# Attention and two quantized convolutions on one core: emitted instruction order, shared single PSUM banks, earlier residual loads

## The chip, the cores and the metric

The kernel runs on one core of a Trainium2 chip. The metric is the device time of one execution in microseconds (us), the median of several runs. A profile is one execution recorded by the hardware profiler; its span runs from the first instruction to the last. The engines are TensorE (PE: matmuls; PEld: its weight loads), VectorE (DVE), ScalarE (ACT), GpSimd (POOL) and SyncE (SP), which issues most transfers. Each takes its own queue of instructions, in the order in which they stand there.

## The reference, cut to what matters

Input `x` is 4 images of 128 channels of 64x64 float32. The first layer is self-attention with four heads of 32 over the 4096 pixels of each image, the second a residual block of two quantized 3x3 convolutions with batch norm.

```python
# layer 0, per image b
x_norm = group_norm(x)                       # 8 groups of 16 channels
q, k, v = split(qkv_w @ x_norm + qkv_b)      # 4 heads, d = 32, 4096 tokens
attn = softmax(q @ k.T * 32 ** -0.5)         # 4096 x 4096 per head
y0 = x + proj_w @ (attn @ v) + proj_b

# layer 1
out = conv3x3(y0, lsq_quantize(w1))          # 128 -> 128 channels, pad 1
out = relu(batchnorm(out))                   # statistics over batch and pixels
out = conv3x3(out, lsq_quantize(w2))
out = relu(batchnorm(out) + y0)              # y0 is the residual
```

## The kernel before: the parts that matter

Attention is cut into 32 blocks of 512 queries (8 for each image, or batch), and a block into 32 steps of 128 keys. One step needs four score matmuls (one for each head, two in a "pair"), two exponentials on ScalarE (128x1024 each), and four weighting matmuls that add the four heads into one PSUM bank, `acc`, each head in 32 of its partitions. The row sums of the exponentials are kept as running sums: 24 steps of a block are added by VectorE into `rsum`, 7 by accumulating transfers into `msum`, whose tiles have one buffer each.

```python
pss = tile_pool(name="pss", bufs=3, space=PSUM)      # score tiles of two banks; later convolution tiles
psa = tile_pool(name="psa", bufs=1, space=PSUM)      # single banks: tag "acc", tag "m"
ppool = tile_pool(name="ppool", bufs=6)              # p, the exponentials of one step
rpool = tile_pool(name="rpool", bufs=1)              # running sums, av, rc
MOVED = range(0, NK - 4, 4)                          # NK = 32
...
def scores(pair):
    ...
    s = pss.tile([P, 2, FB], F32, tag="s")
    for i in range(2):
        h = 2 * half + i
        nc.tensor.matmul(s[:, i, :], k[:, h, c0 : c0 + P], q[:, h, :], start=True, stop=True)
    nc.scalar.activation(pts[step][:, 2 * half : 2 * half + 2, :], s, AF.Exp, scale=SCALE)

def weights(step):
    ...
    if kt == 0:
        acc[n] = psa.tile([P, FB], F32, name=f"acc{n}", tag="acc")
    for h in range(HEADS):
        nc.tensor.matmul(acc[n][h * D : (h + 1) * D, :], v[:, kt % KB, h * D : (h + 1) * D],
                         pt[:, h, :], start=(kt == 0), stop=(kt == NK - 1))
    if kt in MOVED:
        if kt == 0:
            msum[n] = rpool.tile([P, HEADS, FB], F32, tag="rm")
            nc.sync.dma_start(out=msum[n], in_=pt)
        else:
            nc.gpsimd.dma_start(out=msum[n], in_=pt, accum_op=ALU.add)
    elif kt == 2:
        rsum[n] = rpool.tile([P, HEADS, FB], F32, tag="r")
        nc.vector.tensor_tensor(rsum[n], pts[step - 1], pt, ALU.add)
    elif kt > 2:
        nc.vector.tensor_tensor(rsum[n], rsum[n], pt, ALU.add)
```

The program emits three score pairs and one step of weights, then three pairs and two steps, over and over (`for s, w in ((3, 1), (3, 2))`). Side work is hung on the steps of a block: the row sum and output projection of the block before, and, in chunks of 512 pixels, the q, k, v projections that a later block needs.

```python
if before:                                   # the block before
    add(2, "a", before["total"])             # row sum: 8 matmuls into a bank, copied by ScalarE
    for j in range(4):
        add(4 + j, "", lambda j=j: before["invert"](j))
    add(8, "", before["weigh"])
    add(10, "q", before["project"])
    add(11, "", before["store"])
...
def chunk(b, j, kt, fs, loads):              # "q": right after a group of score pairs
    add(kt, "", fs[0])                       # normalize: xn, ScalarE
    add(kt, "q", fs[1])                      # pk matmul
    add(kt + 1, "", fs[2])                   # kh (ScalarE), kl (VectorE), two stores
    add(kt + 1, "q", fs[3])                  # pq matmul
    add(kt + 2, "", fs[4])                   # qh, ql, two stores
    add(kt + 2, "q", fs[5])                  # pv matmuls
    add(kt + 3, "", fs[6])                   # v evacuated and stored
```

Block 0 has 5 such chunks, the other blocks of images 0 to 2 have 24; three more come ahead of block 0. This text is what the program emits. In the kernel before, a scheduler then chooses the order in which instructions stand in each engine's queue.

The convolutions split each input into a high and a low part and add nine shifted matmuls for each. They work on bands of 16 rows with a row at either side; two halves of 8 rows make a band.

```python
def conv(parts, ps, j, w):
    hi, lo = parts
    for part in (lo, hi):
        for tap in range(TAPS):
            nc.tensor.matmul(ps[:, j, :]..., w[:, tap, :], part[:, ...], ...)
...
        prepare(m)
        nc.scalar.copy(dst, ps[:, j, :])
        nc.vector.bn_stats(st[:, b * NB + c, :], dst)
...
a2, c2 = layer(1, second, [])
for b in range(B):
    for j in range(4):
        r = outs.tile([P, Q], F32, tag="r")
        nc.sync.dma_start(out=r, in_=y0[b][:, cs])
        y = outs.tile([P, Q], F32, tag="y")
        nc.vector.scalar_tensor_tensor(y, cv[b][:, cs], a2, r, ALU.mult, ALU.add)
        nc.scalar.activation(y, y, AF.Relu, bias=c2)
        nc.sync.dma_start(out=out[b]...[:, cs], in_=y)
```

Of the kernel before, what the change touches and what calls it, by code (L numbers as in the profile page):

```python
# [22 lines left out]
P = 128  # L23
# [44 lines left out]
def _fast(tc, x, norm_w, norm_b, qkv_wt, qkv_b, proj_wt, proj_b,  # L68
          w1, alpha1, gamma1, beta1, w2, alpha2, gamma2, beta2, out, outer):
    flag = outer.enter_context(tc.tile_pool(name="flag", bufs=1))  # L70
    cnt = flag.tile([1, 1], I32, name="cnt")
    with ExitStack() as ctx:
        _fast_body(ctx, tc, x, norm_w, norm_b, qkv_wt, qkv_b, proj_wt, proj_b,
                   w1, alpha1, gamma1, beta1, w2, alpha2, gamma2, beta2, out, cnt)
    return tc.nc.values_load(cnt[0:1, 0:1], min_val=0, max_val=P)


def _fast_body(ctx, tc, x, norm_w, norm_b, qkv_wt, qkv_b, proj_wt, proj_b,
# [116 lines left out]
    dram = ctx.enter_context(tc.tile_pool(name="dram", bufs=1, space=bass.MemoryType.DRAM))  # L195
    kpool = ctx.enter_context(tc.tile_pool(name="kpool", bufs=NB + 1))
    pss = ctx.enter_context(tc.tile_pool(name="pss", bufs=3, space=PSUM))
    psa = ctx.enter_context(tc.tile_pool(name="psa", bufs=1, space=PSUM))
    y0 = [dram.tile([P, N], F32, name=f"y0_{b}") for b in range(B)]
    att = ExitStack()  # L200
    vpool = att.enter_context(tc.tile_pool(name="vpool", bufs=NB + 1))
# [9 lines left out]
    def f32(t):  # L211
        return t.bitcast(F32)
# [12 lines left out]
    def norm_parts(b, st):  # L225
        mv = small.tile([P, 2], F32, name=f"mv{b}", tag="mv")
        mean = small.tile([P, 1], F32, name=f"mean{b}", tag="mean")
        dv = small.tile([P, 1], F32, name=f"dv{b}", tag="dv")
        gm = {}


        def one():
            nc.vector.bn_aggr(mv, st.rearrange("p j s -> p (j s)"))
            gm[0] = psa.tile([P, FB], F32, name=f"gm{b}", tag="m")
            nc.tensor.matmul(gm[0][:, 0:1], gavg, mv[:, 0:1], start=True, stop=True)

        def two():
            nc.vector.tensor_copy(mean, gm[0][:, 0:1])
            nc.vector.tensor_tensor(dv, mv[:, 0:1], mean, ALU.subtract)
            nc.vector.tensor_tensor(dv, dv, dv, ALU.mult)  # L240
            nc.vector.tensor_tensor(dv, dv, mv[:, 1:2], ALU.add)

        def three():
            gm[1] = psa.tile([P, FB], F32, name=f"gv{b}", tag="m")
            nc.tensor.matmul(gm[1][:, 0:1], gavg, dv, start=True, stop=True)

        def four():
            r = rsqrt_eps(gm[1][:, 0:1], f"gr{b}")
            a = small.tile([P, 1], F32, name=f"ga{b}", tag="ga")
            nc.vector.tensor_tensor(a, r, nw, ALU.mult)  # L250
            c = small.tile([P, 1], F32, name=f"gc{b}", tag="gc")
            nc.vector.tensor_tensor(c, mean, a, ALU.mult)
            nc.vector.tensor_tensor(c, nb, c, ALU.subtract)
            norm[b] = a, c

        return one, two, three, four


# [4 lines left out]
    def project_parts(b, j, xin, wide=False):  # L263
        xn = xpool.tile([P, FB], F32, name=f"xn{b}_{j}", tag="x")
        kq[b, j] = dram.tile([5, P, FB], F32, name=f"kq{b}_{j}")
        ps = {}

        def bank(what):
            if wide:
                t = pss.tile([P, 2, FB], F32, name=f"p{what}{b}_{j}", tag="s")  # L270
                return t[:, 0, :]
            return psa.tile([P, FB], F32, name=f"p{what}{b}_{j}", tag="m")

        def normalize():
            a, c = norm[b]
            nc.scalar.activation(xn, xin(), AF.Identity, bias=c, scale=a)

        def mm(what, o):
            ps[what] = bank(what)
            nc.tensor.matmul(ps[what], wqkv[:, o : o + P], xn, start=True, stop=True)  # L280

        def parts(what, bias, slot):
            hi = stage.tile([P, FB], F32R, name=f"{what}h{b}_{j}", tag=f"{what}h")
            lo = stage.tile([P, FB], F32R, name=f"{what}l{b}_{j}", tag=f"{what}l")
            nc.scalar.activation(hi, ps[what], AF.Identity, bias=bias)  # L285
            nc.vector.scalar_tensor_tensor(lo, ps[what], bias, f32(hi), ALU.add, ALU.subtract)  # L286
            nc.sync.dma_start(out=kq[b, j][slot], in_=f32(hi))
            nc.sync.dma_start(out=kq[b, j][slot + 1], in_=f32(lo))

        def mmv():  # L290
            ps["v"] = bank("v")
            for i in range(KB):
                nc.tensor.matmul(ps["v"][:, i * P : (i + 1) * P], xn[:, i * P : (i + 1) * P],  # L293
                                 wqkv[:, 2 * P : 3 * P], start=True, stop=True)

        def evac_v():
            v = stage.tile([P, FB], F32, name=f"vst{b}_{j}", tag="v")
            nc.vector.tensor_tensor(v.rearrange("p (i f) -> p i f", f=P),
                                    ps["v"].rearrange("p (i f) -> p i f", f=P),
                                    bv.unsqueeze(1).to_broadcast([P, KB, P]), ALU.add)  # L300
            nc.sync.dma_start(out=kq[b, j][4], in_=v)

        return [normalize, lambda: mm("k", P), lambda: parts("k", bk, 0),
                lambda: mm("q", 0), lambda: parts("q", bq, 2), mmv, evac_v]
# [39 lines left out]
    def weights(step):  # L344
        n, kt = divmod(step, NK)
        v = vs[blocks[n][0], kt // KB]
        pt = pts[step]
        if kt == 0:
            acc[n] = psa.tile([P, FB], F32, name=f"acc{n}", tag="acc")
        for h in range(HEADS):  # L350
            nc.tensor.matmul(acc[n][h * D : (h + 1) * D, :], v[:, kt % KB, h * D : (h + 1) * D],  # L351
                             pt[:, h, :], start=(kt == 0), stop=(kt == NK - 1))
        if kt in MOVED:
            if kt == 0:
                msum[n] = rpool.tile([P, HEADS, FB], F32, name=f"rm{n}", tag="rm")
# [4 lines that stand above are left out]
            rsum[n] = rpool.tile([P, HEADS, FB], F32, name=f"r{n}", tag="r")  # L360
# [4 lines that stand above are left out]
    def finish_parts(n):  # L365
# [8 lines left out]


        def total():
            t["l"] = psa.tile([P, FB], F32, name=f"l{n}", tag="m")
            for r in (msum[n], rsum[n]):
                for h in range(HEADS):
                    nc.tensor.matmul(t["l"][h * D : (h + 1) * D, :], ones, r[:, h, :],  # L380
# [14 lines left out]
            t["x"] = load_x(b, qb)  # L395

        def project():
            t["o"] = psa.tile([P, FB], F32, name=f"po{n}", tag="m")
            nc.tensor.matmul(t["o"], wp, av, start=True, stop=True)  # L399

        def store():
# [174 lines left out]
    def conv(parts, ps, j, w):  # L576
        hi, lo = parts
        n = 0
        for part in (lo, hi):
            for tap in range(TAPS):  # L580
                kh, kw = divmod(tap, 3)
                nc.tensor.matmul(ps[:, j, :].rearrange("p (r w) -> p r w", w=W), w[:, tap, :],  # L582
# [24 lines left out]
    nc.vector.tensor_reduce(big, worst, AX.X, ALU.max)  # L607
    bad = small.tile([P, 1], F32, name="bad")
    nc.vector.tensor_scalar(bad, big, LIMIT, None, ALU.is_gt)
    nbad = psa.tile([P, FB], F32, name="nbad", tag="m")  # L610
    nc.tensor.matmul(nbad[0:1, 0:1], bad, ones[:, 0:1], start=True, stop=True)
    nc.vector.tensor_copy(cnt, nbad[0:1, 0:1])
    att.close()

    mid = ctx.enter_context(tc.tile_pool(name="mid", bufs=1))
    outs = ctx.enter_context(tc.tile_pool(name="outs", bufs=4))
    cv = [mid.tile([P, N], F32, name=f"cv{b}") for b in range(B)]

    def batch_norm(i, st):
# [13 lines left out]
    def layer(i, prepare, done):  # L633

        st = mid.tile([P, B * NB, 6], F32, name=f"st{i}")
        for m, (b, g) in enumerate(bandlist):
            ps = done[m] if m < len(done) else conv_tile(i, b, g)
            for j in range(2):
# [4 lines left out]
                c = 2 * g + j  # L643
                dst = cv[b][:, c * FB : (c + 1) * FB]
                nc.scalar.copy(dst, ps[:, j, :])  # L645
                nc.vector.bn_stats(st[:, b * NB + c, :], dst)  # L646
        return batch_norm(i, st)

    def first(m):
# [4 lines left out]

    a1, c1 = layer(0, first, early)

    def relu_band(b, g):
        t = band_tile(f"t1_{b}_{g}")
        inner, lo, hi = border(t, g)
        nc.scalar.activation(inner, cv[b].rearrange("p (h w) -> p h w", w=W)[:, lo:hi, :], AF.Relu,  # L660
                             bias=c1, scale=a1)
        ready[1, b, g] = split(t, f"1_{b}_{g}")

    relu_band(*bandlist[0])
    relu_band(*bandlist[1])

    def second(m):
        if m + 2 < len(bandlist):
            relu_band(*bandlist[m + 2])

    a2, c2 = layer(1, second, [])
    Q = N // 4
    for b in range(B):
        for j in range(4):
            cs = slice(j * Q, (j + 1) * Q)
            r = outs.tile([P, Q], F32, name=f"r{b}_{j}", tag="r")
            nc.sync.dma_start(out=r, in_=y0[b][:, cs])
            y = outs.tile([P, Q], F32, name=f"y{b}_{j}", tag="y")
            nc.vector.scalar_tensor_tensor(y, cv[b][:, cs], a2, r, ALU.mult, ALU.add)  # L679
            nc.scalar.activation(y, y, AF.Relu, bias=c2)  # L680
            nc.sync.dma_start(out=out[b].rearrange("c h w -> c (h w)")[:, cs], in_=y)

# [458 lines left out]
```

## Time and profile before the change

| | |
|---|---|
| time, median of 3 runs | 3111.85 us (3110.21 to 3114.57) |
| span of the profiled execution | 3108.4 us |
| mean granted TensorE clock | 0.981 |

The groups of instructions that cost most, as the page lists them:

| group | count | busy, us | mean of one, ns |
|---|---|---|---|
| exponentials p, ScalarE | 2048 | 1957.7 | 1031 |
| running sum r, VectorE | 736 | 1677.7 | 2280 |
| weighting acc, TensorE | 8192 | 1401.9 | 604 |
| scores s, TensorE | 4096 | 1255.3 | 427 |
| convolution, low part, TensorE | 576 | 151.3 | 407 |
| convolution, high part, TensorE | 576 | 148.3 | 401 |
| accumulating transfers into rm, issued by GpSimd | 192 | | 7.2 us to landing (median) |

"Busy" is the union of the group's intervals; matmuls overlap, so it is less than count times mean. A weighting matmul of one head appears as two records, a score matmul as one. In the views of the trace, the name before the arrow is the tile written, those after it are the tiles read, and the line is that of the kernel. In a wait, the name after the arrow is what ended it. Stages by time: projections of the first chunks to about 45 us, attention to about 2757, first convolution to about 2906, second to about 3056, batch norm, residual and stores to the end.

### The profile page before, as it was taken

What the parts mean: (1) busy time and instruction counts of PE and PEld (TensorE: products, weight loads), DVE (VectorE), ACT (ScalarE), POOL (GpSimd) and SP (SyncE); (2) the same over time, 40 slices, a digit from 0 to 9 for tenths busy, and PEclk for the clock granted to TensorE, in tenths of its full rate; (3) what the DMA queues carried; (4) which work ended last, traced back from release to release, by engine and by line L of the source; (5) the groups of instructions that cost most, each with busy time, mean ns of one, the idle gap of its engine ahead of it and who ended that gap; (6) DMA issues with size and microseconds to landing.
All of it is one profiled execution on the core that took longest, in us unless ns stands there. A gap on an engine that the chain in (4) does not pass through costs nothing.

```text
span 3108.4 us, 36462 instructions
## 1 busy us (share of the span) xinstructions
PE 2967.7 (95%) x14418; PEld 1235.4 (40%) x14418; DVE 2174.8 (70%) x1443; ACT 2130.4 (69%) x2305; POOL 189.9 (6%) x302
## 2 busy tenths in 40 slices
PE   6999999998999999989999999999999999999892
PEld 2333333333334433333333433333333333347672
DVE  4577777766877777777787877778787667764333
ACT  4677778776777778767887778767766777731222
POOL 1000000000000000000000000000000000000000
PEclk9999999999999999999999999999999999999996
DMA  8957655577556555596565655785544545442005
GB/s 235 243 109 176 146 136 136 136 167 164 133 110 165 146 131 130 134 206 156 112 163 141 154 124 124 160 195 117 112 104 88 115 99 109 98 100 60 0 1 190
DMA packets 156274, 413.70 MB, mean 133 GB/s; under 512 B 49776, under 2 KB 50544, under 8 KB 127424
## 3 DMA queue, kind: packets, MB, share of 16 engines
q0 software_dynamic: 28128, 201.67, 32.2%
q1 hardware_dynamic: 127392, 208.58, 24.0%
q8 instruction: 115, 1.88, 0.2%
q10 hardware_dynamic: 576, 1.05, 0.1%
q14 instruction: 63, 0.52, 0.1%
HBM read 117.64 MB, written 58.72 MB: 57 GB/s over the span
## 4 chain that ended last, share of the span: by engine, by line
PE 85%; DMA 7%; DVE 2%; ACT 1%; issue 1%; SPq 0%; POOL 0%; POOLq 0%; ACTq 0%; DVEq 0%
PE acc L351 38%; PE s L339 33%; PE c L582 9%; DMA rm<-p 6%; PE l L380 2%; PE po L399 1%; ACT p L340 1%; PE pq L280 1%; PE pv L293 1%; PE pk L280 1%; DVE y L679 1%; DMA r<-y 1%; DVE rc L387 0%; DMA k<-kq 0%; DVE r L363 0%
## 5 line engine op out<-in xcount | busy, mean ns | idle before, releaser
L340 ACT ACTIVATE p<-s 128x1024 f32<-128x1024 f32 x2048 | 1957.7, 1031 | 622.0 <-PE s L339 517.1
L363 DVE TENSOR_TENSOR r<-r,p 128x2048 f32<-128x2048 f32 x736 | 1677.7, 2280 | 174.9 <-ACT p L340 146.5
L351 PE MATMUL acc<-p,v 128*32 128x512 f32 x8192 | 1401.9, 604 | 0.0
L339 PE MATMUL s<-q,k 128*128 128x512 f32 x4096 | 1255.3, 427 | 31.1 <-ACT p L340 22.0
L339 PEld LDWEIGHTS s<-q,k 128*128 128x128 f32 x4096 | 695.5, 189 | 986.0 <-ACT p L340 492.0
L351 PEld LDWEIGHTS acc<-p,v 128*32 128x32 f32 x8192 | 240.6, 108 | 598.0 <-issue 588.6
L358 POOL DMA_DIRECT2D rm<-p x192 | 164.0, 854 | 2480.7 <-ACT p L340 1705.9
L361 DVE TENSOR_TENSOR r<-p,p 128x2048 f32<-128x2048 f32 x32 | 73.4, 2293 | 271.6 <-PE l L380 241.4
L645 ACT COPY cv<-c 128x512 f32<-128x512 f32 x64 | 37.2, 589 | 206.8 <-PE c L582 196.9
L582 PE MATMUL c<-lo,wq 128*128 128x512 f32 x576 | 151.3, 407 | 13.4 <-DVE lo L431 8.2
L582 PE MATMUL c<-hi,wq 128*128 128x512 f32 x576 | 148.3, 401 | 0.0
L582 PEld LDWEIGHTS c<-lo,wq 128*128 128x128 f32 x576 | 107.8, 192 | 48.0 <-ACT cv L645 11.4
L387 DVE RECIPROCAL rc<-ls 128x128 f32<-128x128 f32 x128 | 118.8, 937 | 6.1 <-ACT ls L383 6.1
L582 PEld LDWEIGHTS c<-hi,wq 128*128 128x128 f32 x576 | 108.3, 188 | 29.8 <-issue 0.8
L646 DVE BATCH_NORM_STATS2 st<-cv 128x6 f32<-128x512 f32 x64 | 43.9, 691 | 103.4 <-ACT cv L645 103.4
L286 DVE SCALAR_TENSOR_TENSOR kl<-pk,bk,kh 128x512 fp32r<-128x512 f32 x32 | 24.0, 750 | 127.4 <-ACT kh L285 126.4
L431 DVE TENSOR_TENSOR lo<-t,hi 128x1188 fp32r<-128x1188 f32 x32 | 44.7, 1396 | 39.4 <-PE c L582 35.7
L380 PE MATMUL l<-rm,ones 128*32 128x512 f32 x256 | 64.2, 617 | 4.2 <-DMA rm<-p 4.2
L430 DVE CAST hi<-t 128x1188 fp32r<-128x1188 f32 x32 | 24.9, 778 | 55.4 <-PE c L582 29.8
L380 PE MATMUL l<-r,ones 128*32 128x512 f32 x256 | 52.3, 597 | 2.0 <-DVE r L363 2.0
L399 PE MATMUL po<-av,wp 128*128 128x512 f32 x64 | 37.2, 664 | 16.1 <-DVE av L390 16.1
L383 ACT COPY ls<-l 128x512 f32<-128x512 f32 x32 | 18.8, 587 | 46.2 <-PE l L380 46.0
(99 smaller groups left out, 595.2 us busy)
## 6 DMA issues: line engine op xcount, KB each, us to landing
rm<-p POOLq DMA_DIRECT2D x192, 1024.0 KB, 7.2
k<-kq SPq DMA_DIRECT2D x128, 256.0 KB, 7.0
q<-kq SPq DMA_DIRECT2D x128, 256.0 KB, 4.7
rm<-p SPq DMA_DIRECT2D x32, 1024.0 KB, 5.6
x<-in_x_dram SPq DMA_DIRECT2D x80, 256.0 KB, 4.0
kq<-kh SPq DMA_DIRECT2D x32, 256.0 KB, 5.5
kq<-kl SPq DMA_DIRECT2D x32, 256.0 KB, 6.1
kq<-qh SPq DMA_DIRECT2D x32, 256.0 KB, 4.8
```

The source lines that it names most:

```text
L280: nc.tensor.matmul(ps[what], wqkv[:, o : o + P], xn, start=True, stop=True)
L339: nc.tensor.matmul(s[:, i, :], k[:, h, c0 : c0 + P], q[:, h, :], start=True, stop=True)
L340: nc.scalar.activation(pts[step][:, 2 * half : 2 * half + 2, :], s, AF.Exp, scale=SCALE)
L351: nc.tensor.matmul(acc[n][h * D : (h + 1) * D, :], v[:, kt % KB, h * D : (h + 1) * D], pt[:, h, :], start=(kt == 0), stop=(kt == NK - 1))
L358: nc.gpsimd.dma_start(out=msum[n], in_=pt, accum_op=ALU.add)
L361: nc.vector.tensor_tensor(rsum[n], pts[step - 1], pt, ALU.add)
L363: nc.vector.tensor_tensor(rsum[n], rsum[n], pt, ALU.add)
L380: nc.tensor.matmul(t["l"][h * D : (h + 1) * D, :], ones, r[:, h, :], start=(r is msum[n]), stop=(r is rsum[n]))
L387: nc.vector.reciprocal(rc[:, cs], t["ls"][:, cs])
L399: nc.tensor.matmul(t["o"], wp, av, start=True, stop=True)
L431: nc.vector.tensor_tensor(lo, f32(t), f32(hi), ALU.subtract)
L582: nc.tensor.matmul(ps[:, j, :].rearrange("p (r w) -> p r w", w=W), w[:, tap, :], part[:, j * RB + kh : j * RB + kh + RB, kw : kw + W], sta ...
```

## The change

The whole fast path is put under a mode in which each engine's queue keeps the order in which the program emits its instructions, in place of the scheduler's. The single PSUM banks of the two tags "acc" and "m", one slot each, become two slots of one tag, so that a new block's `acc` can start in the other bank. The convolutions begin with the high part, which is ready before the low one. Batch-norm statistics are read from PSUM, not from the copy, so that they need not wait for it. The first band of the second convolution is prepared in two pieces, so that its first half can start sooner. The residuals are fetched during the second convolution, half an image at a time, into buffers that stay until the end, and the output is formed in them in place.

```diff
     with ExitStack() as ctx:
+        ctx.enter_context(tc.manual_schedule())
         _fast_body(ctx, tc, x, norm_w, ...)
...
-    psa = ctx.enter_context(tc.tile_pool(name="psa", bufs=1, space=PSUM))
+    psa = ctx.enter_context(tc.tile_pool(name="psa", bufs=2, space=PSUM))
...
-            return psa.tile([P, FB], F32, name=f"p{what}{b}_{j}", tag="m")
+            return psa.tile([P, FB], F32, name=f"p{what}{b}_{j}", tag="a")
...
-            acc[n] = psa.tile([P, FB], F32, name=f"acc{n}", tag="acc")
+            acc[n] = psa.tile([P, FB], F32, name=f"acc{n}", tag="a")
...   (tag "m" to "a" in five more places: gm, gv, l, po, nbad)
-        for part in (lo, hi):
+        for part in (hi, lo):
...
-    outs = ctx.enter_context(tc.tile_pool(name="outs", bufs=4))
...
-                nc.vector.bn_stats(st[:, b * NB + c, :], dst)
+                nc.vector.bn_stats(st[:, b * NB + c, :], ps[:, j, :])
...
-    relu_band(*bandlist[0])
+    relu_band(*bandlist[0], pieces=((0, RB + 2), (RB + 2, BR + 2)))
     relu_band(*bandlist[1])
...   (relu_band takes its rows in pieces: relu, high part, low part for each)
+    HN = N // 2
+    res = {}
+
+    def load_res(b, i):
+        if b < B - 1:
+            t = mid.tile([P, HN], F32, name=f"res{b}_{i}")
+        else:
+            t = f32(stack_tile(f"res{b}_{i}")).rearrange("p h n -> p (h n)")
+        res[b, i] = t
+        nc.sync.dma_start(out=t, in_=y0[b][:, i * HN : (i + 1) * HN])

     def second(m):
         if m + 2 < len(bandlist):
             relu_band(*bandlist[m + 2])
+        if m < 2 * B - 2:
+            load_res(m // 2, m % 2)

     a2, c2 = layer(1, second, [])
+    for i in range(2):
+        load_res(B - 1, i)
     Q = N // 4
     for b in range(B):
         for j in range(4):
+            y = res[b, j // 2][:, (j % 2) * Q : (j % 2 + 1) * Q]
             cs = slice(j * Q, (j + 1) * Q)
-            r = outs.tile([P, Q], F32, name=f"r{b}_{j}", tag="r")
-            nc.sync.dma_start(out=r, in_=y0[b][:, cs])
-            y = outs.tile([P, Q], F32, name=f"y{b}_{j}", tag="y")
-            nc.vector.scalar_tensor_tensor(y, cv[b][:, cs], a2, r, ALU.mult, ALU.add)
+            nc.vector.scalar_tensor_tensor(y, cv[b][:, cs], a2, y, ALU.mult, ALU.add)
             nc.scalar.activation(y, y, AF.Relu, bias=c2)
             nc.sync.dma_start(out=out[b]...[:, cs], in_=y)
```

More of the change, by code (lines that the diff above doesn't have):

```diff
@@ L233, in one @@
             nc.vector.bn_aggr(mv, st.rearrange("p j s -> p (j s)"))
-            gm[0] = psa.tile([P, FB], F32, name=f"gm{b}", tag="m")
+            gm[0] = psa.tile([P, FB], F32, name=f"gm{b}", tag="a")
             nc.tensor.matmul(gm[0][:, 0:1], gavg, mv[:, 0:1], start=True, stop=True)
@@ L243, in three @@
         def three():
-            gm[1] = psa.tile([P, FB], F32, name=f"gv{b}", tag="m")
+            gm[1] = psa.tile([P, FB], F32, name=f"gv{b}", tag="a")
             nc.tensor.matmul(gm[1][:, 0:1], gavg, dv, start=True, stop=True)
@@ L376, in total @@
         def total():
-            t["l"] = psa.tile([P, FB], F32, name=f"l{n}", tag="m")
+            t["l"] = psa.tile([P, FB], F32, name=f"l{n}", tag="a")
             for r in (msum[n], rsum[n]):
@@ L397, in project @@
         def project():
-            t["o"] = psa.tile([P, FB], F32, name=f"po{n}", tag="m")
+            t["o"] = psa.tile([P, FB], F32, name=f"po{n}", tag="a")
             nc.tensor.matmul(t["o"], wp, av, start=True, stop=True)
@@ L609, in _fast_body @@
     nc.vector.tensor_scalar(bad, big, LIMIT, None, ALU.is_gt)
-    nbad = psa.tile([P, FB], F32, name="nbad", tag="m")
+    nbad = psa.tile([P, FB], F32, name="nbad", tag="a")
     nc.tensor.matmul(nbad[0:1, 0:1], bad, ones[:, 0:1], start=True, stop=True)
@@ L655, in _fast_body, with relu_rows, relu_band @@
     a1, c1 = layer(0, first, early)
[L657 to L660, printed above, removed]
-                             bias=c1, scale=a1)
-        ready[1, b, g] = split(t, f"1_{b}_{g}")
-    relu_band(*bandlist[0])
-    relu_band(*bandlist[1])
+    def relu_rows(b, g, t, r0, r1):
+        inner, lo, hi = t["inner"]
+        a, e = max(r0 + g * BR - 1, lo), min(r1 + g * BR - 1, hi)
+        nc.scalar.activation(inner[:, a - lo : e - lo, :],
+                             cv[b].rearrange("p (h w) -> p h w", w=W)[:, a:e, :], AF.Relu,
+                             bias=c1, scale=a1)
+        nc.vector.tensor_copy(t["hi"][:, r0:r1, :], f32(t["t"])[:, r0:r1, :])
+        nc.vector.tensor_tensor(t["lo"][:, r0:r1, :], f32(t["t"])[:, r0:r1, :],
+                                f32(t["hi"])[:, r0:r1, :], ALU.subtract)
+    def relu_band(b, g, pieces=((0, BR + 2),)):
+        t = {n: band_tile(f"{n}1_{b}_{g}") for n in ("t", "hi", "lo")}
+        t["inner"] = border(t["t"], g)
+        for r0, r1 in pieces:
+            relu_rows(b, g, t, r0, r1)
+        ready[1, b, g] = t["hi"], t["lo"]
+    relu_band(*bandlist[0], pieces=((0, RB + 2), (RB + 2, BR + 2)))
+    relu_band(*bandlist[1])
+    HN = N // 2
[7 more added lines that the diff above has]
+        nc.sync.dma_start(out=t, in_=y0[b][:, i * HN : (i + 1) * HN])
     def second(m):
```

## The prediction

> **What bounds the kernel now.** I read the page's busy shares first, then the granted clock by stage, then the matmul timeline of one block, then the waits. TensorE is busy 95% of the span, the other two compute engines 69 to 70%:
>
> ```profile
> PE 2967.7 (95%) x14418; PEld 1235.4 (40%) x14418; DVE 2174.8 (70%) x1443; ACT 2130.4 (69%) x2305; POOL 189.9 (6%) x302
> ```
>
> A table by stage shows where this holds. Columns: stretch in us, its length, then busy time and instructions of each engine, granted clock, DMA share, GB/s.
>
> ```profile
> 660.00:760.00 100.00, 86.43 (x408) 33.32 (x406) 64.96 (x39) 60.42 (x66) 5.15 (x6) 0.93 0.82 188
> 760.00:1320.00 560.00, 560.00 (x2856) 217.60 (x2848) 427.62 (x252) 441.61 (x478) 37.49 (x42) 1.00 0.58 135
> 2290.00:2660.00 370.00, 368.79 (x1715) 126.44 (x1713) 266.12 (x153) 270.01 (x281) 21.27 (x25) 1.00 0.46 101
> 3056.00:3109.00 53.00, 0.00 (x0) 0.00 (x0) 21.61 (x22) 18.36 (x16) 0.55 (x1) 0.51 0.78 278
> ```
>
> Attention (about 45 to 2757) is TensorE without a gap, save the stretches where the next batch's keys are loaded: 660 to 760 loses 13.6 us at a DMA share of 0.82. The end, 3056 to 3109, has no matmul. A block of 32 steps has about 402 matmul records (128 score, 256 weighting, 16 row-sum, 2 projection): at 560/2856 = 0.196 us each that is 79 us, at 370/1715 = 0.216 it is 87 us in the last batch.
>
> But "busy" here is not work at full rate. The matmul timeline (start, busy, line, tile, records; one head's weighting is two records) has two cycles of three steps, side by side:
>
> ```profile
> 1494.82 1.65 PE L339 MATMUL s<-q,k 128*128 128x512 f32 x6
> 1496.40 1.92 PE L351 MATMUL acc<-p,v 128*32 128x512 f32 x16
> 1498.25 1.67 PE L339 MATMUL s<-q,k 128*128 128x512 f32 x6
> 1499.86 1.06 PE L351 MATMUL acc<-p,v 128*32 128x512 f32 x8
> 1500.85 1.19 PE L339 MATMUL s<-q,k 128*128 128x512 f32 x4
> 1501.98 1.04 PE L351 MATMUL acc<-p,v 128*32 128x512 f32 x2
> 1502.95 0.73 PE L339 MATMUL s<-q,k 128*128 128x512 f32 x2
> 1503.62 1.92 PE L351 MATMUL acc<-p,v 128*32 128x512 f32 x14
> 1505.46 1.63 PE L339 MATMUL s<-q,k 128*128 128x512 f32 x6
> 1507.03 1.06 PE L351 MATMUL acc<-p,v 128*32 128x512 f32 x8
> 1508.02 1.20 PE L339 MATMUL s<-q,k 128*128 128x512 f32 x4
> ```
>
> From 1494.82 to 1500.85 three steps take 6.03 us: six scores, two whole steps of weighting, six scores, one whole step. From 1500.85 to 1508.02 the same three steps take 7.17 us, because one head of a step (x2) was put between scores. That lone head holds TensorE from 1501.98 to 1502.95, 0.97 us; all four heads at 1507.03 take 0.99. A split costs 7.17 - 6.03 = 1.14 us.
>
> **What the Trainium skill says.** "TensorEngine Tiling (Array Packing)", Key Properties: tiles work in parallel, and a change of tiling mode drains the engine. The trace agrees: four 32-column heads take the time of one, and 6 scores in 1.6 us against 2 in 0.67 leave about 0.2 us for each change. "TensorE: Matmul & The Clock Gate", Part 3, The mechanism: matmuls start and end strictly in program order. So one that waits holds those behind it; I use this for the chunks below. "DMA: Bandwidth & Descriptors", Where 436 GB/s comes from: about 358 GB/s between HBM and SBUF for one core. The final stretch here averages 278 with its idle gaps; for stores alone I allow 358 to 410.
>
> **The change, part by part.**
>
> *Whole steps.* Of the 1024 weighting steps in the scheduled program, 341 are split; in the emitted order none is. If TensorE stays the bound: 341 x 1.14 = -389 us. The last batch has denser splits, shown by 87 us a block against 79: 8 x 7 blocks = -56.
>
> *ScalarE comes near.* Exponentials are spaced 0.952 us, six in a cycle: 5.71 us under 6.03, and two 0.59 us copies per block. The three score slots must turn over: walking one cycle, the third score of the second group waits about 0.2 us for its slot. 32 x 10.7 cycles x 0.2 = +68.
>
> *Block start.* The running sums have one buffer each. The new block's first sum copy waits for the row-sum matmuls at step 2, then takes its 5.6 us landing, and the exponential six steps on needs that p buffer: by my walk +1.5 us per block, 32 x 1.5 = +48.
>
> *Projection chunks, the largest cost.* All of k, q, v projections share the one PSUM slot that acc leaves free, now as before. The emitted order puts pk and pq, or pq and pv, next to each other, or pk right behind the normalize that feeds it. Walk of the first kind, from the start of a three-score group: scores end 1.6, pk 2.5; but kh stands behind three exponentials and ends 4.8, kl (0.75) 5.6, so pq starts 5.6 and not 2.5; pq and a weighting step to 7.5; scores to 9.1; qh after three more exponentials 11.9, ql 12.6, so pv starts at 12.8; pv 1.1 and two weighting steps, 15.7. Without the chunk 6.2. So 9.5 us, of which 3.0 are the chunk's own matmuls; the other two kinds gave 8.9 and 9.1. 29 chunks inside blocks x about 6 = +174. The scheduler had hidden nearly all of that.
>
> *Other in-order waits.* Group-norm averages of the next batch wait on VectorE on the TensorE queue: 3 batches x 5 = +15. The quantization tasks issue a load and use it at once, and VectorE's 24 sums (2.28 us each) then run late: +27. Key loads: blocks that change batch stay near DMA-bound, so of the gain there about 45 us is lost, against 37 us of idle TensorE in the three such stretches now: +8.
>
> Attention: -389 - 56 + 68 + 48 + 174 + 15 + 27 + 8 = -105.
>
> *Convolutions.* Statistics read from PSUM run beside the copy instead of after it (0.6 us at each of two ends). The high part first and a first band of ten rows shorten the restart (relu 1.3, cast 0.78, subtract 1.40) by about 3. The last attention block's tail, where TensorE idles about 5 us between 2760 and 2905, should close up. Together -8.
>
> *The end.* The waits of the last stretch name the residual load:
>
> ```profile
> L679 DVE SCALAR_TENSOR_TENSOR y<-cv,ba,r 128x1024 f32<-128x1024 f32 x16 | 20.3, 1283 | 23.3 <-DMA r<-y 21.2 <-DMA out_dram<-y 2.0
> ```
>
> With the residuals there and no output slots to wait for, 16 x 1.28 = 20.5 us on VectorE remain, then a relu (1.15) and one landing (3.1). A 0.524 MB store in 1.28 us is 410 GB/s; at 358 it is 1.46, 23.4 us for 16. So -24, or -21.
>
> Sum: -105 - 8 - 24 = -137, 2975. Each wait left out of such walks adds time, none takes it away; I add 15 and say **2990 us**.
>
> **Rivals.**
> 1. *The in-order waits eat the gain of the whole steps.* For: TensorE at 6.03, ScalarE at 5.71 and VectorE at 61 us of work in a block of 70 are all so close that a wait on one is soon a wait on all, and p and score buffers hold only a few steps. Against: in the whole-step cycle above TensorE ran on without a gap. At +3.5 us per block and 12 us a chunk the attention stands where it was: about 3080.
> 2. *DMA becomes the bound.* Moving p into the running sum lands in 7.2 us (median), once every four steps; four steps shrink from 9.6 to 8.3 us. For: with key loads landings already last 10 to 14 us. Against: elsewhere the DMA share is 0.58. If landings rise by 1.5 us everywhere, six per block: 32 x 9 x half = +140, time about 3130.
> 3. *The chunk waits overlap with work I counted twice*, and whole steps give their full -389: about 2880.
> 4. *The store end is hidden by nothing and gains less*: it can move the result by 5 us only.
>
> **Range and chances.** The block length is uncertain by 1.5 us (48 us), a chunk by 2 us (58), DMA stretches by 40: together about 85, somewhat skewed upward. Range 2900 to 3085. Faster by 2% means under 3050: 0.77. Within 2%: 0.18. Slower: 0.05.
>
> **What would show it.** Right: no lone x2 weighting groups, weighting busy time down from 1402 to about 980 us, plain blocks near 70 us, TensorE gaps ahead of pq and pv naming kl, ql or kh, ScalarE waits for TensorE behind them; an end of about 29 us after the last matmul instead of 53. Wrong: if plain blocks still take 79, the split was not what held the pace, and ScalarE waiting for p buffers (releaser "rm<-p") would say that the DMA did. If the end does not shrink to about 30 us, the stores, not the loads, were its bound.

## The result, and the profile after

The changed kernel takes 3191.11 us (median of 4 runs, 3179.06 to 3197.23); before, 3111.45 us measured beside it. The ratio is 1.025, with a 95% interval of 1.0218 to 1.0282: slower by 2.5%. The forecast was 2990 us and faster. The profiled execution is the quickest of the four, with a span of 3177.3 us and a mean granted TensorE clock of 0.94 (before: 3108.4 us and 0.981).

The page's busy shares of the changed kernel:

```profile
PE 2731.6 (86%) x14418; PEld 1226.8 (39%) x14418; DVE 2196.2 (69%) x1445; ACT 2099.9 (66%) x2306; POOL 184.4 (6%) x302
```

TensorE has lost 236 us of busy time for the same matmuls, as the change was to bring, and yet the span grew by 69. The table by stage says where (same columns as before; first the attention before the change, then in the changed kernel first convolution, second convolution, end, attention):

```profile
37.70:2757.30 2719.60, 2672.59 (x13204) 1011.46 (x13204) 2014.19 (x1236) 2042.54 (x2194) 172.66 (x208) 0.99 0.61 141
...
2803.30:2974.40 171.10, 146.37 (x598) 109.10 (x596) 62.49 (x74) 19.74 (x34) 2.27 (x27) 0.99 0.31 82
2974.40:3147.30 172.90, 144.16 (x576) 108.59 (x576) 59.21 (x72) 38.72 (x49) 4.25 (x41) 0.98 0.04 13
3147.30:3177.30 30.00, 0.00 (x0) 0.00 (x0) 21.17 (x22) 18.36 (x16) 0.55 (x1) 0.56 0.71 281
37.20:2802.80 2765.60, 2428.61 (x13206) 1001.83 (x13206) 2041.12 (x1254) 2015.84 (x2198) 167.32 (x208) 0.94 0.60 138
```

| stage | before, us | after, us | difference | forecast |
|---|---|---|---|---|
| attention, first score to first convolution matmul | 2719.6 | 2765.6 | +46 | -105 |
| both convolutions with batch norm | 298.3 | 344.0 | +46 | -8 |
| from the last batch norm to the end | 52.8 | 30.0 | -23 | -24 |

In the attention TensorE was idle 47 us before (2719.6 less 2672.6 busy) and is now idle 337. The list of waits of the changed kernel (engine, line, what for: total us, times, longest) names three causes:

```profile
ACT p L341 <- DMA rm<-p: 220.7, 78, 9.7
PE s L340 <- ACT p L341: 121.0, 87, 8.4
PE pk L281 <- ACT xn L277: 82.0, 22, 7.7
PE pq L281 <- DVE kl L287: 58.9, 19, 5.8
PE pv L294 <- DVE ql L287: 54.4, 19, 3.4
PE c L583 <- DVE st L646: 46.1, 30, 5.0
```

The first is ScalarE with no free p buffer, because a transfer still reads the old one. It was there before, at less than a third. The second is TensorE waiting for ScalarE to free a score tile, which is where such a delay reaches it. Before:

```profile
ACT p L340 <- DMA rm<-p: 62.1, 30, 5.7
PE s L339 <- ACT p L340: 22.0, 26, 3.5
```

The next three are TensorE at the head of a projection that stands next to what it depends on: 195 us together, and about 5 before. The last is the convolutions. Of these, only the three of the projections were given their due in the forecast. The chain of work that ended last has changed too: the accumulating transfers have 22% of it and not 6% (shares of the span by line, before and after):

```profile
PE acc L351 38%; PE s L339 33%; PE c L582 9%; DMA rm<-p 6%; PE l L380 2%; PE po L399 1%; ACT p L340 1%; PE pq L280 1%; PE pv L293 1%; PE pk L280 1%; DVE y L679 1%; DMA r<-y 1%; DVE rc L387 0%; DMA k<-kq 0%; DVE r L363 0%
DMA rm<-p 22%; PE s L340 21%; PE acc L352 20%; PE c L583 8%; ACT p L341 5%; DVE r L364 2%; PE l L381 2%; DMA q<-kq 1%; PE pk L281 1%; PE pv L294 1%; DMA k<-kq 1%; PE pq L281 1%; DVE st L646 1%; DVE res L704 1%; ACT cv L645 1%
```

One case of each cause follows.

**A chunk.** Timeline of the changed kernel, cut to the lines that matter:

```profile
464.00 1.66 PE L340 MATMUL s<-q,k 128*128 128x512 f32 x6
...
465.50 1.02 PE L281 MATMUL pk<-xn,wqkv 128*128 128x512 f32 x2
467.55 0.70 ACT L286 ACTIVATE kh<-pk,bk 128x512 fp32r<-128x512 f32 x1
...
468.29 0.75 DVE L287 SCALAR_TENSOR_TENSOR kl<-pk,bk,kh 128x512 fp32r<-128x512 f32 x1 [3.61 <-ACT kh L286]
...
469.09 1.12 PE L281 MATMUL pq<-xn,wqkv 128*128 128x512 f32 x2 [2.57 <-DVE kl L287]
...
476.18 1.16 PE L294 MATMUL pv<-wqkv,xn 128*128 128x128 f32 x8 [3.38 <-DVE ql L287]
477.26 1.92 PE L352 MATMUL acc<-p,v 128*32 128x512 f32 x16
479.12 1.66 PE L340 MATMUL s<-q,k 128*128 128x512 f32 x6
...
485.32 1.66 PE L340 MATMUL s<-q,k 128*128 128x512 f32 x6
```

pk is done by 466.5; kh stands behind three exponentials until 467.55; pq follows 2.57 us late, pv 3.38 us late. From group to group 15.1 us pass, where the forecast's walk of this kind has 15.7. The next cycle, without a chunk, takes 6.20 us.

**The start of a block.** In the same block, some 25 us earlier:

```profile
437.85 0.86 POOL L359 DMA_DIRECT2D rm<-p  x1 [39.53 <-ACT p L341]
...
447.85 4.00 ACT L341 ACTIVATE p<-s 128x1024 f32<-128x1024 f32 x4 [1.98 <-DMA rm<-p]
...
455.35 4.69 ACT L341 ACTIVATE p<-s 128x1024 f32<-128x1024 f32 x5 [3.51 <-DMA rm<-p]
...
456.43 0.74 PE L340 MATMUL s<-q,k 128*128 128x512 f32 x2 [2.20 <-ACT p L341]
...
458.36 1.93 PE L352 MATMUL acc<-p,v 128*32 128x512 f32 x8
```

The first accumulating transfer, issued at 437.85, lands 9.9 us later, as the next block's queries are loaded beside it; the next one can only then start, ScalarE waits for both, and TensorE's scores wait 2.20 us behind the second. The last line is a second thing to see: one weighting step takes 1.93 us where it took 1.06. The granted clock of this stretch, the third figure from the end, is 0.72:

```profile
455.40:460.20 4.80, 3.59 (x12) 0.86 (x12) 4.10 (x3) 4.64 (x5) 0.86 (x1) 0.72 1.02 233
```

**A convolution.** Copy, statistics, and the matmul behind them:

```profile
2843.64 0.59 ACT L645 COPY cv<-c 128x512 f32<-128x512 f32 x1 [3.71 <-PE c L583]
2844.26 0.70 DVE L646 BATCH_NORM_STATS2 st<-c 128x6 f32<-128x512 f32 x1 [1.49 <-ACT cv L645]
2845.01 2.42 PE L583 MATMUL c<-hi,wq 128*128 128x512 f32 x9 [1.41 <-DVE st L646]
```

The statistics start when the copy has ended, though they no longer read it, and the matmuls of the band's second half start when the statistics have ended. Such a step of 1.8 us from one matmul to the next (0.24 is ordinary) stands between the two halves of each of the 30 bands that are not begun during attention.

### The profile page after: what moved, and what is told of

Read it like the earlier page. It is cut to its first block, busy times and chain, and to the rows that moved or that the text cites. A ratio compares the mean times of both kernels' runs of the same rounds, so it can differ in the third digit from the quotient of the medians.

```text
span 3177.3 us, 36327 instructions
## 1 busy us (share of the span) xinstructions
PE 2731.6 (86%) x14418; PEld 1226.8 (39%) x14418; DVE 2196.2 (69%) x1445; ACT 2099.9 (66%) x2306; POOL 184.4 (6%) x302
## 4 chain that ended last, share of the span: by engine, by line
PE 53%; DMA 24%; ACT 6%; DVE 6%; issue 5%; ACTq 0%; POOLq 0%; POOL 0%; DVEq 0%; SPq 0%
DMA rm<-p 22%; PE s L340 21%; PE acc L352 20%; PE c L583 8%; ACT p L341 5%; DVE r L364 2%; PE l L381 2%; DMA q<-kq 1%; PE pk L281 1%; PE pv L294 1%; DMA k<-kq 1%; PE pq L281 1%; DVE st L646 1%; DVE res L704 1%; ACT cv L645 1%
## 5 line engine op out<-in xcount | busy, mean ns | idle before, releaser
L341 ACT ACTIVATE p<-s 128x1024 f32<-128x1024 f32 x2048 | 1927.5, 1036 | 668.1 <-PE s L340 405.4
L340 PE MATMUL s<-q,k 128*128 128x512 f32 x4096 | 1237.5, 431 | 145.4 <-ACT p L341 121.0
L352 PE MATMUL acc<-p,v 128*32 128x512 f32 x8192 | 1084.7, 633 | 0.0
L352 PEld LDWEIGHTS acc<-p,v 128*32 128x32 f32 x8192 | 203.1, 112 | 512.6 <-issue 503.0
L646 DVE BATCH_NORM_STATS2 st<-c 128x6 f32<-128x512 f32 x64 | 44.7, 698 | 204.2 <-ACT cv L645 203.8
L583 PEld LDWEIGHTS c<-hi,wq 128*128 128x128 f32 x576 | 108.2, 193 | 94.5 <-DVE st L646 59.4
L281 PE MATMUL pk<-xn,wqkv 128*128 128x512 f32 x64 | 49.3, 862 | 82.0 <-ACT xn L277 82.0
L287 DVE SCALAR_TENSOR_TENSOR ql<-pq,bq,qh 128x512 fp32r<-128x512 f32 x32 | 24.0, 749 | 115.3 <-ACT qh L286 115.2
L281 PE MATMUL pq<-xn,wqkv 128*128 128x512 f32 x64 | 42.2, 746 | 58.9 <-DVE kl L287 58.9
L294 PE MATMUL pv<-wqkv,xn 128*128 128x128 f32 x256 | 40.5, 307 | 54.4 <-DVE ql L287 54.4
L294 PEld LDWEIGHTS pv<-wqkv,xn 128*128 128x128 f32 x256 | 36.3, 213 | 69.4 <-DVE ql L287 66.6
```

The lines of the kernel that those rows point to most:

```text
L646: nc.vector.bn_stats(st[:, b * NB + c, :], ps[:, j, :])
```

## Experiments

All times are medians of 4 runs; ratios are to the kernel before, run beside them, with 95% intervals. Block lengths are taken from the start of one block's first score matmul to the next's, the last block's to its last score matmul. Where the text gives a gain on the changed kernel, it is the difference to its 3191.11 us, measured at another time; the kernel before read 3110.3 to 3111.8 us each time.

### Undoing the order

```diff
-        ctx.enter_context(tc.manual_schedule())
```

> The changed kernel with the scheduler's order back, everything else of the change kept. Theory A (the emitted order's waits cost more than its whole weighting steps bring): the attention goes back to about 2720 us and the split weighting groups return (about 1400 us busy); with the shorter end (-22) the time is about 3090. Rival (statistics from PSUM cost in the convolutions whatever the order): each convolution stays some 20 us longer, time about 3130.

Measured: 3131.52 us, ratio 1.0066 (1.0049 to 1.0083). Neither: the convolutions go back to 152 and 148 us, so statistics from PSUM cost nothing where the scheduler puts other matmuls between; the weighting is busy 1457 us (before the change 1402). But the attention takes 2759 us and not 2720. The expected mechanism missed that, so the one thing left in attention, the PSUM tags, was undone as well:

```diff
-        ctx.enter_context(tc.manual_schedule())
-    psa = ... bufs=2 ... ; tag="a"
+    psa = ... bufs=1 ... ; tag="acc" for acc, tag="m" for the others
```

> The scheduler's order and the two separate one-slot tags back; what is left of the change are the convolution parts and the earlier residuals. Theory (the one tag of two slots let the scheduler choose a worse attention order): the attention goes back from 2760 to about 2720 us, time about 3090. Rival (the convolution parts or chance in the scheduler's choice): stays at 3131.

Measured: 3089.72 us, ratio 0.9932 (0.9916 to 0.9949), attention 2719.6 us, as before the change. What follows: the convolution parts and the earlier residuals by themselves are worth 21 us, all of it at the end of the kernel; and the shared tag of two slots costs 42 us when the scheduler orders the instructions. Which of the scheduler's choices costs them stays open. The same tags were tried in the emitted order:

> The changed kernel with the two one-slot tags back, emitted order kept. A new block's acc must then wait for the copy of the one before, behind ScalarE's three exponentials: about 1 us in each of 31 blocks, time about 3220. Rival (the other bank is never the last thing waited for): 3191, no difference.

Measured: 3194.40 us, ratio 1.0275 (1.0258 to 1.0292). The rival had the time right, since 3 us are within the spread of the runs, but not its reason. With one bank TensorE does wait for the copy, while the changed kernel has no such line:

```profile
PE acc L352 <- ACT av L374: 16.5, 11, 1.5
```

The 16.5 us don't reach the end. This run and the one before it differ in the order alone: it costs 105 us (3089.72 to 3194.40). In the profiled executions, 101 us apart, 56 of them fall into the attention and 45 into the convolutions.

### Spreading the chunks

```diff
-            add(kt, "", fs[0])            # and so on: two of the three matmuls side by side
+            add(kt - 2, "", fs[0])        # chunks of block 0 stay as they were
+            for i in range(3):
+                add(kt + 2 * i, "q", fs[1 + 2 * i])
+                add(kt + 2 * i, "", fs[2 + 2 * i])
```

> Emitted order, but the 24 projection chunks for a later batch are spread: normalize two steps earlier, pk, pq and pv two steps apart, each evacuated right behind. Theory A (TensorE waiting in order for kh, kl, ql and xn): 24 x 5 to 6 us come back, time about 3055. Theory B (p buffers held by accumulating transfers set the pace): the waits only move to the p buffers, at most 40 us come back, about 3150.

Measured: 3014.27 us, ratio 0.9685 (0.9669 to 0.9701). 177 us come back, more than theory A had. Blocks with two chunks fall from 95.2 us (mean of six) to 78.5, blocks with one (mean of nine) from 84.2 to 76.5: 8 us a chunk. The waits of this kernel:

```profile
PE pk L281 <- ACT xn L277: 26.7, 9, 5.9
PE pq L281 <- DVE kl L287: 9.6, 5, 3.0
PE pv L294 <- DVE ql L287: 8.4, 3, 3.4
```

They fell from 195 to 45 us, 25 of the rest being block 0's. ScalarE's wait for p buffers stayed at 220.8 us: theory B is not what the chunks cost, but a second cost beside it. Weighting and projections, the same instructions, are also busy 42 us less in all (1216.7 to 1174.8): with the long waits gone fewer of them run at a lowered clock (see below).

### The transfers

```diff
-            add(2, "", lambda: load_q(b, qb + 1))
+            add(20, "", lambda: load_q(b, qb + 1))
```

> Emitted order, the load of the next block's queries moved from step 2 to step 20, away from the first accumulating transfers of a block. Theory B (these transfers land in 10 us and not 7 because the query load runs beside them, and ScalarE then waits for the p buffer): 3 to 4 us in each of 28 blocks, time about 3090. Theory A: under 20 us, about 3175.

Measured: 3153.41 us, ratio 1.0126 (1.0103 to 1.0149). 38 us, between the two theories. The first accumulating transfer of a block lands in 7.1 us (median of 32 blocks) and not in 9.8, as theory B has it, and ScalarE's wait for p buffers falls by 60 us, to 160.7.

```diff
-                nc.gpsimd.dma_start(out=msum[n], in_=pt, accum_op=ALU.add)
+                nc.gpsimd.dma_start(out=msum[n][:, 0:2, :], in_=pt[:, 0:2, :], accum_op=ALU.add)
```

> Emitted order, but the accumulating transfers move only two of four heads: half the row sums of those steps are left out, the output is not the reference's. Theory B: ScalarE's 221 us of waiting for p buffers held by transfers nearly vanish, and 130 to 180 us come back: about 3030. Theory A: the chunks cost what they cost, at most 50 us: about 3145.

Measured: 3074.70 us, ratio 0.9874 (0.9858 to 0.9891). With half of each accumulating transfer left out, 116 us come back, again between the two; the wait for p buffers falls to 88.5 us, and blocks without side work to about 69 us (before this step 70 to 75). So the transfers are a cost of some 116 us at least, the chunks one of 177.

### The convolutions

```diff
-            for j in range(2):
-                if m >= len(done):
-                    conv(ready[i, b, g], ps, j, wq[i])
+            if m >= len(done):
+                for j in range(2):
+                    conv(ready[i, b, g], ps, j, wq[i])
+            for j in range(2):
                 if j == 0:
                     prepare(m)
```

> Emitted order, but in the convolutions both halves of a band are emitted before the copies and statistics of either, so that the second half's matmuls don't stand behind the first half's readers. Theory (30 waits of 1.8 us between halves, 0.24 us of them ordinary): the two convolutions together lose about 47 us, time about 3144. Rival (VectorE or ScalarE paces the convolutions): the wait moves to the next band, under 10 us, about 3182.

Measured: 3132.34 us, ratio 1.0054 (1.0034 to 1.0073). The kernel gains 59 us, and the two convolutions take 291.3 us and not 344.0: -53 us. None of the 1.8 us steps is left.

```diff
-                nc.vector.bn_stats(st[:, b * NB + c, :], ps[:, j, :])
+                nc.vector.bn_stats(st[:, b * NB + c, :], dst)
```

> Emitted order, statistics read from the copy again and not from PSUM, nothing else changed. Theory (the statistics follow the copy anyway, and reading PSUM only makes the next half's matmuls wait for them too): each of 30 waits falls from 1.8 to about 1.1 us, -22 us, about 3169. Rival (reading PSUM frees the chain as it was meant to): the same or slower, 3191 or more.

Measured: 3156.99 us, ratio 1.0142 (1.0125 to 1.0159). The steps fall from 1.80 to 1.07 us, the convolutions to 316.7 us, -27. So of the 53 us that the halves' order brings back, 27 are the wait for statistics read from PSUM and the rest the wait for the copy. Both hang on the emitted order: under the scheduler the convolutions took 300 us with the same statistics.

### Together, and the splits put back

> The spread chunks, the later query load and the joined convolution halves in one kernel, emitted order. If the three costs are independent: 3191 - 177 - 38 - 47, about 2930. If the chunks and the query load hid the same p-buffer waits: about 2960.

The three edits in one kernel, the joined kernel: 2956.08 us, ratio 0.9505 (0.9489 to 0.9521). It falls where the second forecast had it. The three gains measured alone, 177 + 38 + 59, would give 2917, so 39 us of them overlap; which of them was not separated.

```diff
+        # one step in three: one head's weighting before the third score pair, three after it
+            for _ in range(2): scores(...)
+            begin(at["step"])
+            s = 1
```

> The joined kernel with the splits put back: in one step of three, one head's weighting matmul is emitted before the third score pair and the other three heads after it, as the scheduler had it. Theory (a lone head costs 1.14 us of TensorE, and TensorE is the bound): up to 341 x 1.14 = 389 us more than the joined kernel, at least 300 if some falls into waits on p buffers. Rival (in the emitted order ScalarE and the p buffers set the pace, not TensorE): under 150 us more.

Measured: 3156.82 us, ratio 1.0143 (1.0126 to 1.0160): 201 us more than the joined kernel, between the two. The matmul timeline is the scheduler's again, with the lone head at 0.98 us:

```profile
2703.25 1.21 PE L340 MATMUL s<-q,k 128*128 128x512 f32 x4
2704.39 1.05 PE L351 MATMUL acc<-p,v 128*32 128x512 f32 x2
2705.37 0.73 PE L340 MATMUL s<-q,k 128*128 128x512 f32 x2
2706.03 1.06 PE L362 MATMUL acc<-p,v 128*32 128x512 f32 x6
```

Weighting is busy 1404.8 us in its two groups (first two lines), against 1061.7 in the joined kernel (third line):

```profile
L362 PE MATMUL acc<-p,v 128*32 128x512 f32 x7510 | 1040.6, 609 | 6.5 <-ACT p L341 6.5
L351 PE MATMUL acc<-p,v 128*32 128x512 f32 x682 | 364.2, 616 | 0.0
L352 PE MATMUL acc<-p,v 128*32 128x512 f32 x8192 | 1061.7, 619 | 10.4 <-ACT p L341 10.4
```

These 343 us of TensorE's time are 1.0 us for each of 341 splits, where 1.14 was forecast. Blocks without side work take 79.6 us (five of them, 78.9 to 80.3; joined 68.8 to 75.1). But blocks with key loads stay at 99 to 104 in both. Only 201 us reach the end, under the 300 of the theory: TensorE's idle time in the attention falls from 222 to 123 us as the splits fill it, so TensorE is not the bound everywhere.

### A faster version

The blocks with key loads were left at 99 to 104 us. In these alone, 4 sums were moved by transfers and not 7:

```diff
-        if kt in MOVED:
+        if moved(n, kt):        # range(0, NK - 4, 8) in blocks that load the next batch's keys
```

> The joined kernel, with 4 and not 7 of the sums moved by transfers in the three blocks that load the next batch's keys; VectorE adds the other three. Theory (in these blocks accumulating transfers land in 11 to 14 us beside the key loads and hold the p buffers): each falls from about 102 to 85 us, -50 us, about 2905. Rival (VectorE, with 3 x 2.28 us more, takes their place): under 15 us.

Measured: 2907.76 us, ratio 0.9355 (0.9339 to 0.9371). -48 us; the three blocks fall from 102.2, 104.0 and 99.4 to 85.0, 87.3 and 84.4, as expected. VectorE carried the three extra sums.

```diff
-        few = qb == NB - 1 and b + 1 < B
+        few = n == 0 or (qb == NB - 1 and b + 1 < B)
-        if b == B - 1 and qb in (1, 2):
-            for i, f in enumerate(qtasks[:7] if qb == 1 else qtasks[7:]):
-                add(12 + 2 * i, "", f)
+        if b == B - 1 and qb in (1, 2, 3, 4):
+            for i, f in enumerate(qtasks[2 * qb - 2 : 2 * qb]):
+                add(13 + 9 * i, "", f)
```

> The same with block 0 treated likewise, and the quantization in pairs of tasks over four blocks and not seven tasks in one. Theory: block 0 from 116 to about 105, the two blocks with quantization from 91 and 93 to about 78, four blocks touched instead, in all about -20 to -30 on the kernel with fewer moved sums. Rival: block 0 is held by its own five chunks and the quantization only moves: no gain.

Measured: 2893.27 us, ratio 0.9294 (0.9279 to 0.9310), the fastest here and 9.3% under the changed kernel. The gain is 14 us, under the 20 to 30 expected. The two blocks with quantization fall from 91.7 and 91.0 to 77.8 and 80.4, while the next two become 3 and 8 longer: 14 us in all. That these are the 14 of the medians is not shown, as the two profiled executions differ by only 2 us. Block 0 stays at 115: there the rival was right.

## Why the prediction was wrong

By its own steps, against the 2990 forecast:

1. *Splits cost TensorE 1.14 us each, and TensorE is the bound: nearly right, and right only in part.* A split costs 1.0 us. Weighting is busy 1084.7 us and not 1401.9, though not the 980 forecast; a cycle of three steps is 6.2 us (6.0 and the 0.2 forecast for the score slot). Blocks without side work are 70 to 75 us, forecast 70; the same five took 79 to 94 before, and putting splits back makes them 79.6. There TensorE is the bound, with 2 us of idle time a block; in the other kinds of blocks it idles 5 to 25. The row-sum matmuls, which the scheduler had split too, fall from 116.5 to 66.6 us busy, which the forecast had not counted.

2. *Chunks, +174: the wait was right, the clock was left out.* The walk of one kind was within 0.6 us. In the 15 blocks that have chunks and no key loads (21 chunks), spreading them took away 112 us of TensorE's idle time, 5.4 us a chunk where about 6 were forecast. But these blocks became 169 us shorter, 8 us a chunk. Nearly all the rest is a clock that the walk left at full speed.

   The clock records of the trace have two values, full and half, and in the attention each stretch at half lasts 3.41 us or a multiple of it. A weighting step that lies in one takes 1.94 us (median of 39), the others 1.07 (median of 934). In the attention of the changed kernel, all 26 gaps of 3.4 us or more in TensorE's work were followed by half clock within 3.4 us, 38 of 51 gaps of 2.5 to 3.4 us, 7 of 14 of 1.5 to 2.5, and none of 29 of 0.2 to 1.5. The Trainium skill, "TensorE: Matmul & The Clock Gate", Part 1, What's actually happening, states that the clock is halved after about 3.4 us without work; here shorter gaps often did it too, such as the 2.20 us shown above, while the chunk shown kept the full clock with gaps of 2.57 and 3.38 us.

   If half of TensorE's busy time in such stretches is lost, the 15 blocks lost 70 us to the clock, and 18 with the chunks spread: an estimate from the trace's clock records, as are the figures on the clock below.

3. *Accumulating transfers, +48 at block starts and +8 at key loads: too small.* ScalarE's wait for their p buffers rose from 62 to 221 us, and TensorE's for a score tile from 22 to 121. The three key-load blocks took 105.2, 103.6 and 103.8 us, forecast 94.5 (70.5 + 9 + 15); before they took 104.5, 104.9 and 98.9, so nothing of the gain arrived there; the three after them 78.4 on average, forecast 70.5. Giving the key blocks fewer transfers brought 48 us, halving all of them 116. What failed in these two terms is where they put the waits. Rival 2, landings 1.5 us longer everywhere, did not hold, as the median rose only from 7.2 to 7.4 us. But the first accumulating transfer of a block, now beside the load of queries, lands in 9.8 us (median; before 7.0), and five of the six in a key-load block take 11 to 14 (before 8 to 14), whatever TensorE gains.

4. *Convolutions, -8: the sign was wrong; +46.* "Statistics read from PSUM run beside the copy instead of after it" failed. They still follow it, and they now also hold TensorE. The skill's "PSUM — Partial Sum Buffer", PSUM bank collisions raise a hardware error, says that two engines must be kept apart on one bank, ScalarE's and VectorE's reads included; in the trace 61 of the 64 statistics are released by the end of their copy. That matmuls of the second half wait for readers of the first, in another bank of the same two-bank tile, the order alone decides: with both halves emitted first, 53 us come back. Only the shorter restart held: TensorE idles 6.0 us between the two convolutions, before 8.2.

5. *The end, -24: right.* 52.8 to 30.0 us; VectorE does its 16 pieces without a gap. From 3152 to 3172 us the transfers move 376 GB/s, above the 358 that the forecast cites and below the 410 that it also allowed for.

The convolutions account for 54 of the miss, and experiments show why. The attention accounts for 151 (+46 for -105): in block lengths, chunk blocks about 82 more than forecast, key-load blocks 29, the blocks after them 24, quantization blocks 11. In TensorE's time the 46 us are three terms:

| attention, TensorE | forecast, us | measured, us |
|---|---|---|
| busy, as at full clock (-389 - 56 + 68) | -377 | -358 |
| idle (+48 + 174 + 15 + 27 + 8) | +272 | +290 |
| lost to the lowered clock | 0 | +115 |

The 68 stand with the busy time, as the 6.20 us of a cycle are busy throughout. The last term and the first rest on the estimate: TensorE is busy at half clock for 277 us of the attention, before for 47, and half of each is taken as lost. The two terms that were forecast came out within 20 us each, partly by luck. In the busy time, the row-sum's 50 us made up for splits that cost less than forecast. In the idle time, the 15 us for group-norm averages, which did not come (TensorE waits 12 us for them in all, as before), made up for the transfers. So the step that failed in the attention is that every walk ran TensorE at full clock, waits or not; the 15 us added for waits left out are far from covering it. No run here holds the clock fixed, so the 115 us are not shown by an experiment of their own. That weighting and projections, the same instructions, lost 42 us of busy time when the chunk waits went is the nearest to one: the estimate has 42 there as well.

## What to carry to other kernels

Whole groups of column-tiled matmuls are worth keeping together, but an emitted order must be written for the queue: between an instruction and the one that needs its result, put as much other work as the slowest engine's backlog, as two steps did here. When the fastest engine is sped up, look at once at what it had been hiding: here a 7 us transfer that holds a buffer, and that lands in 10 us and more beside other loads. Count TensorE's gaps twice, once for the gap and once for the clock after it. And a bank read by two engines was read here by one after the other, so that moving a reader from the copy to the bank lengthened the time until the bank was free.

## What was not expected of the hardware

Waiting costs TensorE twice: after the longer waits it resumes at half clock, a weighting step of 1.94 us for 1.07, and the mean granted clock of the attention fell from 0.99 to 0.94. The accumulating transfer's landing is 7 us alone and 10 to 14 us beside loads of queries or keys. And one PSUM tag of two slots, in place of two tags of one, cost 42 us under the scheduler and nothing in the emitted order: a pool's shape can change what a scheduler chooses more than what the chip waits for.
